# A graph-attention layer with expert feed-forward on one core: the experts' steps get written slots, twelve products of zeros stand ahead of the transposes of the maxima's ends, and the block records start five side steps later

## The chip, the cores and the metric

The kernel runs on one core of a Trainium2 chip. The metric is the device time in microseconds of one execution; less is better. The engines are TensorE (PE; its weight loads are shown as PEld), VectorE (DVE), ScalarE (ACT), GpSimd (POOL) and SyncE (SP). Each works through its own instructions in the order in which the program wrote them, and waits on semaphores for the others.

## The reference

The input is a table `x` of 30000 nodes by 256 features and 510000 edges (`src`, `dst`, a relation of 8 for each), sorted by `dst`. Cut to what matters:

```
xn = layernorm(x)
feat[r, n, h] = xn[n] @ conv_weights[r, h]            # 8 relations, 4 heads of 64
e  = leaky_relu(el[src, type] + er[dst, type])        # one score for each edge and head
m  = segment_max(e, dst);  ex = exp(e - m[dst])
h  = segment_sum(ex / segment_sum(ex) * feat[type, src], dst) + h_bias
x  = x + h
xn = layernorm(x)
gates = softmax(xn @ gW + gb);  top 2 of 4 experts, weights softmaxed again
x  = x + shared_mlp(xn) + sum of the two chosen experts' mlp(xn)
```

## The kernel before

**Stage A** (to about 1740 us) makes `feat`. For each of 235 tiles of 128 nodes it normalizes, transposes, multiplies with all conv weights on TensorE (`group`, L305) and stores the rows to HBM. Beside it runs `side`, a list of generators of which `aside()` advances the first by one `yield`: once a tile while there are three of them, twice a tile afterwards. The second generator, `places` (L490 on), reads the sorted edge records of 12 blocks at a time. Its inner `fetch(k)` issues 12 loads on SP, one for each block, with an address that is read from a register; `fetch(0)` is followed by one `yield`, and after that DVE reads what it brought (`key`, L534).

**Stage B** (about 1740 us to the end) goes over 253 blocks of edges: 252 of 16 times 128 edges, and a last one of 18 times 128. A block covers at most 128 destination nodes. The loop runs over `t` and, inside, over six slots `c`. Work on several blocks is interleaved in the written order of one slot:

- slot 0: loads for block t+2 (SP), the 15 indirect gathers of `feat` rows for block t+1 (POOL, L933; the sixteenth part comes from a stage in HBM), flags for t+1 (ACT copies), the residual of block t-2 (DVE)
- slot 1: two transposes (`pn`) and their copy `through` (ACT), then DVE's `scores(t)`, which ends in two scans that write `fb` (L1033, L1034)
- slot 2: `turn_ends(t)`: TensorE transposes the ends of both scans into the PSUM tile `t1` (L1040, L1041)
- slot 3: `across(t)`: DVE scans over the partitions (L1047, L1048), which reads `t1` and `through`
- slot 4: `turn_back(t)`: two transposes to `t2` (L1055, L1056); DVE's `dest_select(t+2)` (L970)
- slot 5: DVE's `softmax(t)` (L1062 to L1022), ACT's `exps(t)` (L1071, L1072), DVE's first `weigh` of the block (L1079), then `finish(t-1)`: `den` and `ho` (L1104 to L1107) from the PSUM tile `po`

In every slot there are also a part of `sums(t-1)` on TensorE (L1086: one-hot times gathered rows, summed in `po`), a part of `weigh` and `dest_pick` on DVE, of `dest_expand` on TensorE (L987, bf16) and of `onehot` on ACT (L1010, L1011). `po`, `t1`/`pn`/`t2` (one tag, `sm`) and the experts' `pf`/`pw`/`pg` (one tag, `pc`) have one PSUM buffer each.

**The experts.** Four blocks make a group of 512 nodes. When the residual of the fourth is done (slot 0), `Experts.steps()` gives 22 steps: `spread` (ACT's square root, L727), `scale` 0 and 2 (DVE), `turn` 0 and 1 (transposes; ACT copies `xT`, L744), `shared1(0)`, `gates`, `shared1(1)`, four `experts1` (the first holds `choose`, 14 small DVE operations), `shared2`, two `experts2`, two `weigh`, `turn_gates` (transposes the gate weights; ACT copies `wT`, L844), and four `last` (L851 to L854), which need `wT`. Before, the steps go into the list `todo`, and each slot takes one of it: steps 0 to 21 sit in slots 0 to 21 of the 24 slots of four blocks. A step may return a second half; it is kept in `late` and runs at the start of the next slot. So `last(t)` makes the product in one slot, and DVE adds it to `og` (L857) at the start of the next.

Of the kernel before, what the change touches and what calls it, by code (L numbers as in the profile page):

```python
# [11 lines left out]
BF16 = mybir.dt.bfloat16  # L12
# [9 lines left out]
P = 128  # L22
D = 256
R = 8
H = 4
# [15 lines left out]
T = 4  # L41
# [12 lines left out]
def kernel(  # L54
# [26 lines left out]
    nc = tc.nc  # L81
# [94 lines left out]
    for i in range(NPEN + 1):  # L176
        f = wf.tile([P, H, U if i < NPEN else UL], F32, name=f"penf{i}")
# [44 lines left out]
    with ExitStack() as cx:  # L222
# [268 lines left out]
        def places(cl):  # L491
# [19 lines left out]
            def fetch(k):  # L511
                if k == len(batches):
                    return
                b0, n = batches[k]
                rc = rcs[k] = kp.tile([P, GB, UW, 4], I32, name="rcb")
                for b in range(n):
                    lo = nc.values_load(lo_sb[0:1, b0 + b:b0 + b + 1], engines={SP}, min_val=0, max_val=E)
                    r = rec[ds(lo, CAP), :].rearrange("(p u) f -> p (u f)", u=U)
                    nc.sync.dma_start(rc[:, b].rearrange("p u f -> p (u f)"),
                                      bass.AP(tensor=r.tensor, offset=r.offset, ap=[[4 * U, P], [1, 4 * UW]]))  # L520

            fetch(0)
            yield
            done = None
            for k, (b0, n) in enumerate(batches):
                fetch(k + 1)
# [99 lines left out]
        with tc.manual_schedule():  # L626
# [27 lines left out]
            while slot < 16:  # L654
                attention(slot, ab)
                slot += 1
            cl.close()
            side = [edge_records(cl), places(cl), expert_weights()]
            ahead = first_rows()

# [41 lines left out]
    class Experts:  # L702
# [8 lines left out]
        def steps(self):  # L711
# [5 lines left out]
                    + [lambda i=i: self.weigh(i) for i in range(2)]  # L717
                    + [self.turn_gates] + [lambda t=t: self.last(t) for t in range(self.n)])

        def stats(self, t):  # L720
            st = self.pool.tile([P, 6], F32, name="c_st")
            nc.vector.bn_stats(st[:M], self.x1[:M, t, :])
            nc.vector.bn_aggr(self.mv[:M, t, :], st[:M])
# [138 lines left out]
    with ExitStack() as cx:  # L862
        cp = cx.enter_context(tc.tile_pool(name="cb", bufs=1))
# [15 lines left out]
        NCH = 6  # L879
        flat = "p h u -> p (h u)"  # L880
        blk = {}

        class Block:

# [152 lines left out]
        def turn_ends(t):  # L1037
            s = blk[t]
            s.t1 = ps_p.tile([H, 2, P], F32, name="t1", tag="sm")
            nc.tensor.transpose(s.t1[:, 0, :], s.f[:, :, s.u - 1], ident)  # L1040
            nc.tensor.transpose(s.t1[:, 1, :], s.b[:, :, 0], ident)  # L1041

# [44 lines left out]
                                 s.ft[:, u].rearrange("p h d -> p (h d)"), start=u == 0, stop=u == s.u - 1)  # L1087

        groups = {}
        todo = []  # L1090
        late = []

        def put(t, rows_t):

            if t < NBLK:
                n0 = nc.values_load(n0_sb[0:1, t:t + 1], engines={SP}, min_val=0, max_val=N - P)
                nc.sync.dma_start(out[ds(n0, P), :], rows_t)
            else:
                nc.sync.dma_start(out[N - P:N, :], rows_t)
# [9 lines left out]
        def residual_sum(t):  # L1109
            s = blk.pop(t)  # L1110
            q, j = divmod(t, T)
            n = min(T, NBLK + 1 - q * T)
            if j == 0:
                x1 = x1p.tile([P, T, D], F32, name="x1")
                groups[q] = Experts(xc, ph_p, pc_p, x1, n, lambda i, r, q=q: put(q * T + i, r))
            x1 = groups[q].x1
            nc.vector.tensor_add(x1[:, j, :], s.ho.rearrange("p h d -> p (h d)"), s.xt)
            groups[q].stats(j)
            if j == n - 1:
                todo.extend(groups.pop(q).steps())  # L1120

        with tc.manual_schedule():
            for t in range(-2, NBLK + 12):
                def at(f, b, *a):
                    if 0 <= b <= NBLK:
                        f(b, *a)
                for c in range(NCH):
                    while late:  # L1130
                        late.pop()()
                    if c == 0:
                        at(load, t + 2)
                        at(gather, t + 1)
                        at(flags, t + 1)
                    if c == 1:
                        at(flags_across, t + 1)
                    if c == 2:
                        at(turn_ends, t)
                    if c == 3:  # L1140
                        at(across, t)
                    if c == 4:
                        at(turn_back, t)
                    if c == 5:
                        at(softmax, t)
                        at(exps, t)
                    if c < NCH - 1:
                        at(weigh, t - 1, c + 1)
                    if c < 4:
                        at(dest_pick, t + 1, c)  # L1150
                    if c == 0:
                        at(residual_sum, t - 2)
                    if c == 1:
                        at(scores, t)
                    if c == 4:
                        at(dest_select, t + 2)
                    if todo:
                        after = todo.pop(0)()
                        if after:
                            late.append(after)  # L1160
                    if c == 5:
                        at(weigh, t, 0)
                        at(dest_expand, t + 2, 0)
                    if c < 3:
                        at(dest_expand, t + 1, c + 1)
                    at(onehot, t, c)
                    at(sums, t - 1, c)
                    if c == 5:
                        at(finish, t - 1)
            assert not todo and not groups and not late  # L1170


    again = nc.values_load(bad[0:1, 0:1], min_val=0, max_val=1)
# [57 lines left out]
    with ExitStack() as cx:  # L1231
        cp = cx.enter_context(tc.tile_pool(name="cg", bufs=1))
# [128 lines left out]
    with ExitStack() as cx:  # L1361
# [3 lines left out]
        with tc.For_i(0, again * NQ) as q:  # L1365
# [7 lines left out]
            for step in g.steps():  # L1373
                after = step()
# [30 lines left out]
```

## Time and profile before

| what | value |
|---|---|
| median of 10 runs | 6656.92 us (6650.02 to 6666.61) |
| the profiled execution's own time | 6647.23 us |
| its span, first to last instruction | 6645.6 us |
| mean granted TensorE clock | 0.967 |
| busy share: PE, DVE, ACT, POOL | 90%, 81%, 52%, 61% |
| gathers of stage B | 3798, mean 953 ns |
| `sums` products | 8100 instructions, 2214.0 us busy |

"Idle before" is the time that an engine stood ahead of an instruction, and the releaser is the instruction whose semaphore ended it. Granted clock is the share of full speed that the TensorE throttle gave. The profiled execution is 9.7 us shorter than the median.

### The profile page before, as it was taken

To read this page: it belongs to the slowest core of one execution; us is meant where nothing else is said; L and a number is where in the kernel's file an instruction comes from. 1 tells how busy PE (TensorE), PEld (TensorE's weight loads), DVE (VectorE), ACT (ScalarE), POOL (GpSimd) and SP (SyncE) were. 2 spreads that over 40 slices of the span, in tenths; PEclk is the share of its full clock that TensorE was granted. 3 is DMA by queue.
4 is the path that set the end of the run, shared out by engine and by line. 5 is a ranking of instruction groups with operands and counts; after the bars stand their busy time and mean duration, and the time that the engine had idled before them with its cause. 6 is when DMAs were issued, how large, how long until landed. Compare 5 with 4: busy or idle time off the path is not lost. (4 is left out here: it accounts for less than half of the span.)

```text
span 6645.6 us, 96556 instructions
## 1 busy us (share of the span) xinstructions
PE 5978.2 (90%) x25254; PEld 3836.3 (58%) x25255; DVE 5353.9 (81%) x13882; ACT 3428.1 (52%) x9511; POOL 4084.0 (61%) x4327
## 2 busy tenths in 40 slices
PE   9999999999788888888888888888888888888888
PEld 5555555555456566555555565655656555655555
DVE  5555777644588888999999989899999998888886
ACT  2222222222355666665666656666666666566664
POOL 1111111166677777777777777777777777777772
PEclk9999999999899999999999999999999999999998
DMA  6666777799755555555555555555555555555552
GB/s 226 227 211 182 232 234 232 241 342 348 248 154 160 166 161 159 161 157 167 162 160 160 159 161 166 160 161 159 158 167 161 162 158 156 165 159 157 162 156 64
DMA packets 761458, 1209.52 MB, mean 182 GB/s; under 512 B 241639, under 2 KB 599790, under 8 KB 730686
## 3 DMA queue, kind: packets, MB, share of 16 engines
q1 hardware_dynamic: 565453, 663.56, 31.3%
q0 software_dynamic: 194400, 539.40, 29.4%
q8 instruction: 206, 3.38, 0.2%
q14 instruction: 359, 2.93, 0.1%
q10 hardware_dynamic: 1040, 0.26, 0.0%
HBM read 818.57 MB, written 384.23 MB: 181 GB/s over the span
## 5 line engine op out<-in xcount | busy, mean ns | idle before, releaser
L933 POOL DMA_INDIRECT ft<-feat,rk x3798 | 3619.7, 953 | 1198.3 <-issue 465.1
L1086 PE MATMUL po<-ft,oh 128*128 128x260 f32 x8100 | 2214.0, 408 | 153.1 <-DVE ho L1107 139.7
L1086 PEld LDWEIGHTS po<-ft,oh 128*128 128x128 f32 x8100 | 1512.5, 201 | 416.2 <-ACT ends L955 144.3
L305 PE MATMUL ps<-w,xT 128*128 128x448 f32 (+1 forms) x4700 | 1710.2, 519 | 10.5 <-DVE xT L294 8.7
L1079 DVE TENSOR_TENSOR ft<-ft,p 128x768 f32<-128x768 f32 x1518 | 1289.9, 850 | 183.0 <-ACT ft L1072 183.0
L1010 ACT ACTIVATE oh<-icol,rk 128x128 f32<-128x128 f32 x4032 | 1329.1, 389 | 0.0
L305 PEld LDWEIGHTS ps<-w,xT 128*128 128x128 f32 x4700 | 876.4, 191 | 699.6 <-issue 607.9
L307 ACT COPY fo<-ps 128x448 f32<-128x448 f32 (+1 forms) x711 | 378.3, 533 | 1080.6 <-PE ps L305 990.7
L1011 ACT ACTIVATE oh<-oh 128x384 f32<-128x384 f32 x1518 | 740.2, 488 | 48.1
L987 PEld LDWEIGHTS <-ohT 128*128 128x128 bf16 x4050 | 390.9, 158 | 402.0 <-issue 308.4
L1000 DVE TENSOR_REDUCE e<-ere 128x16 f32<-128x384 f32 (+1 forms) x1012 | 561.5, 555 | 34.8
L998 DVE TENSOR_TENSOR ere<-pe,rk 128x384 f32<-128x384 f32 x1008 | 551.7, 547 | 1.3 <-PE pe L987 1.3
L798 PE MATMUL ph<-xT,v 128*128 128x512 f32 (+1 forms) x1024 | 484.3, 596 | 1.0 <-ACT h L799 0.6
L1071 ACT ACTIVATE p<-e 128x64 f32<-128x64 f32 (+1 forms) x253 | 71.2, 281 | 751.9 <-DVE e L1022 742.9
L987 PE MATMUL pe<-erp,ohT 128*128 128x96 bf16 x4050 | 434.0, 232 | 26.1 <-DVE ohT L970 25.5
L307 DVE COPY fo<-ps 128x448 f32<-128x448 f32 (+1 forms) x464 | 242.8, 528 | 211.6 <-PE ps L305 205.8
L294 DVE COPY xT<-ptr 128x256 f32<-128x256 f32 x229 | 97.3, 425 | 368.6 <-PE ptr L292 366.4
L615 POOL DMA_INDIRECT fr<-feat,lowc x252 | 239.9, 952 | 169.2 <-DMA stage<-fr 70.6
L970 DVE TENSOR_SCALAR ohT<-dr,rowid 128x2064 bf16<-128x2064 int16 (+1 forms) x253 | 324.2, 1281 | 3.5 <-DMA feat<-fo 3.0
L274 POOL TENSOR_TENSOR xb<-xg,hb 128x1024 f32<-128x1024 f32 (+1 forms) x59 | 141.9, 2405 | 287.7 <-DMA xg<-in_x_dram 145.3
L851 PE MATMUL pf<-w,h 128*128 128x256 f32 x506 | 169.4, 418 | 148.8 <-ACT wT L844 111.7
L1040 PE MATMUL t<-ident,fb 128*4 128x128 f32 x253 | 69.8, 276 | 237.4 <-DVE fb L1033 237.4
(206 smaller groups left out, 6966.5 us busy)
## 6 DMA issues: line engine op xcount, KB each, us to landing
feat<-fo SPq DMA_DIRECT2D x234, 1040.0 KB
dr<-dk_d SPq DMA_DIRECT2D x252, 516.0 KB
ft<-feat,rk POOLq DMA_INDIRECT x3798
stage<-fr SPq DMA_DIRECT2D x63, 520.0 KB
ft<-stage SPq DMA_DIRECT2D x252, 130.0 KB
xt<-xb_d SPq DMA_DIRECT2D x253, 128.0 KB
out_dram<-og SPq DMA_DIRECT2D x253, 128.0 KB
xb_d<-xb SPq DMA_DIRECT2D x58, 512.0 KB
```

What stands on the lines that cost most here:

```text
L305: nc.tensor.matmul(ps, t["xT"][:, k, :], w[:, k, c0:c1], start=k == 0, stop=k == 1)
L307: eng(t["fo"][:, h0:h1, :HD], ps[:, :n].rearrange("p (a d) -> p a d", d=HD))
L798: nc.tensor.matmul(ps[:, :self.w], lhs, rhs, start=i == 0, stop=i == len(pairs) - 1)
L933: nc.gpsimd.indirect_dma_start(out=s.ft[:, u].rearrange("p h d -> p (h d)"), out_offset=None, in_=feat[:, :], in_offset=bass.IndirectOffse ...
L970: nc.vector.tensor_scalar(ohT[:, :3 * s.dw].rearrange("n (i e) -> n i e", i=3), s.dr[:, :, :s.dw], rowid[:, t:t + 1], None, op0=ALU.is_equal)
L987: nc.tensor.matmul(pe[:, u - u0].rearrange("p f r -> p (f r)"), s.ov[:, u, :], s.erp.rearrange("n h k r -> n (h k r)"), start=True, stop=True)
L998: nc.vector.tensor_mul(ere, s.pe[:, :u1 - u0], s.th[:, u0:u1, None, :].to_broadcast([P, u1 - u0, H * 3, R]))
L1000: nc.vector.tensor_reduce(s.e[:, :, u0:u1].rearrange("p h u -> p u h"), ere.rearrange("p u (h k) r -> p u h (k r)", h=H), AX.X, ALU.add)
L1010: nc.scalar.activation(s.oh[:, u, :], icol, AF.Abs, bias=s.nd[:, u:u + 1])
L1011: nc.scalar.activation(s.oh[:, u0:u1], s.oh[:, u0:u1], AF.Relu, bias=1.0, scale=-1.0)
L1079: nc.vector.tensor_mul(fc, fc, pc[:, :, None].to_broadcast([P, (u1 - u0) * H, HD]))
L1086: nc.tensor.matmul(s.po.rearrange("n h d -> n (h d)"), s.oh[:, u, :], s.ft[:, u].rearrange("p h d -> p (h d)"), start=u == 0, stop=u == s. ...
```

## The change

Three edits. `places` yields six times after `fetch(0)` instead of once. The steps get written slots: step number i of a group runs in slot `SLOTS[i]`, counted from the slot in which the group's fourth residual is made; a group's last four steps fall into the first four slots of the following group, where that group's own step comes first. `late` is now taken from its front. And `turn_ends` first makes twelve products of a 128 by 4 by a 128 by 256 slice of a bf16 tile of zeros into `t1`, which the two transposes then overwrite.

```diff
@@ places
             fetch(0)
-            yield
+            for _ in range(6):
+                yield
@@ class Experts
+        SLOTS = (0, 1, 2, 4, 5, 7, 8, 9, 10, 11, 12, 13, 14, 15, 16, 18, 19, 21, 24, 25, 26, 27)
@@ stage B
+        zeros = cp.tile([P, 2 * P], BF16, name="zeros")
+        nc.vector.memset(zeros, 0.0)
@@ def turn_ends(t)
             s.t1 = ps_p.tile([H, 2, P], F32, name="t1", tag="sm")
+            for _ in range(12):
+                nc.tensor.matmul(s.t1.rearrange("h i p -> h (i p)"), zeros[:, :H], zeros, start=True, stop=True)
             nc.tensor.transpose(s.t1[:, 0, :], s.f[:, :, s.u - 1], ident)
@@ def residual_sum(t)
-                todo.extend(groups.pop(q).steps())
+                first = free[0] = max((t + 2) * NCH, free[0])
+                free[0] += T * NCH
+                for i, f in zip(Experts.SLOTS, groups.pop(q).steps()):
+                    plan.setdefault(first + i, []).insert(0, f)
@@ the loop
                     while late:
-                        late.pop()()
+                        late.pop(0)()
...
-                    if todo:
-                        after = todo.pop(0)()
+                    for f in plan.pop(t * NCH + c, ()):
+                        after = f()
                         if after:
                             late.append(after)
```

More of the change, by code (lines that the diff above doesn't have):

```diff
@@ L1089 @@
         groups = {}
-        todo = []
+        plan = {}
         late = []
+        free = [0]
         def put(t, rows_t):
@@ L1169 @@
                         at(finish, t - 1)
-            assert not todo and not groups and not late
+            assert not plan and not groups and not late
     again = nc.values_load(bad[0:1, 0:1], min_val=0, max_val=1)
```

## The prediction

> **What bounds the kernel now.** First the page's shares, which name no single engine:
>
> ```profile
> PE 5978.2 (90%) x25254; PEld 3836.3 (58%) x25255; DVE 5353.9 (81%) x13882; ACT 3428.1 (52%) x9511; POOL 4084.0 (61%) x4327
> ```
>
> So I read stage B by itself: the instructions of the score line and of the gather line, with their first and last start.
>
> ```profile
> L1027 DVE TENSOR_TENSOR e<-e,ft x253: 259/266/296, 1764.7 to 6563.1; 128x64 f32<-128x64 f32 x126, 128x72 f32<-128x72 f32 x1
> ```
> ```profile
> L933 POOL DMA_INDIRECT ft<-feat,rk x3798: 943/949/1195, 1744.2 to 6542.7; - x200
> ```
>
> The 252 steps from first to last score take 4798.4 us: 19.04 a block, 76.16 a group of four. Next, DVE's waits from 1800 to 6550 us:
>
> ```profile
> DVE ft L1079 <- ACT ft L1072: 180.2, 249, 2.0
> DVE og L857 <- PE pf L854: 77.2, 131, 1.6
> DVE den L1104 <- PE po L1086: 18.7, 59, 0.5
> ```
>
> DVE hardly ever stands. It waits 0.71 once a block for the exponentials, and for TensorE 95.9 us in 62.4 groups: 1.54 a group. With 10.8 us for gathers (0.17) all else is DVE's own work: 76.16 - 1.71 = 74.45 a group. DVE sets the pace, and what can change is its waits. TensorE stands several us a group, but it is in order and its waits end on DVE.
>
> The timeline of one group (slot 0 of the `last` block is 4652.00, of the block before it 4634.01) shows where DVE waits, and what I price with:
>
> ```profile
> 4606.77 0.22 PE L1055 MATMUL t<-ident,carf 4*128 4x4 f32 x1
> ...
> 4607.67 0.59 ACT L744 COPY xT<-ph 128x512 f32<-128x512 f32 x1
> ...
> 4609.71 1.28 ACT L1071 ACT_TABLE_LOAD   x1
> ...
> 4611.31 0.28 ACT L1071 ACTIVATE p<-e 128x64 f32<-128x64 f32 x1 [0.32 <-DVE e L1022]
> ...
> 4659.40 0.60 PE L851 MATMUL pf<-w,h 128*128 128x256 f32 x2
> ...
> 4661.42 0.45 PE L987 MATMUL pe<-erp,ohT 128*128 128x96 bf16 x4
> 4661.52 0.42 DVE L857 TENSOR_TENSOR og<-pf,x 128x256 f32<-128x256 f32 x1 [0.55 <-PE pf L854]
> ...
> 4664.77 0.42 DVE L857 TENSOR_TENSOR og<-pf,x 128x256 f32<-128x256 f32 x1 [0.30 <-PE pf L854]
> ```
>
> POOL is a second floor: in the same timeline gathers start 1.253 apart (0.95 busy, 0.30 of issue), 60 a group, 75.2. Over the stage its 3797 steps need 4758 of the 4798.5 they took. So however short DVE's waits become, the gathers end at most 41 us earlier; the last score, 20.4 after the last gather, could close up by some 15 more.
>
> Last, stage A. TensorE is full there but for one hole:
>
> ```profile
> 575.00:580.00 5.00, 0.00 (x0) 0.00 (x0) 0.12 (x1) 0.00 (x0) 0.00 (x0) 0.63 0.17 33
> 580.00:585.00 5.00, 2.23 (x3) 1.17 (x4) 4.36 (x14) 0.71 (x2) 0.00 (x0) 0.50 0.17 33
> ```
>
> DVE stood 12.43 us ahead of `key` for the records of `fetch(0)`, TensorE 8.66 behind it, and then ran some 10 us at half clock.
>
> **Part one, the yields.** Five more side steps, two a tile of about 7.5 us, put `key` 19 us later than 567.5; the records were there at 579.9. The wait goes: 8.7, and half of 10.2 for the clock, 14 us less. The twelve loads keep SP as before; `fetch(1)` and all of `places` move back by some 11, far from the end of stage A. **-14.**
>
> **Part two, the slots.** DVE's sum stays. Of TensorE's step work one `last` is 2.02 (4659.40 to 4661.42), a 512-column step 1.72. The four `last` move from the third block of a group's 24 slots after the first into the first block of the next group, beside `scale` (0.84 and 0.65 on DVE), `turn`, and the exponential's table load, which follows the square root. The wait for `wT` (1.83 on TensorE, the start of the lateness in the `last` block) goes, since `turn_gates` is now three slots ahead. The half-clock stretches behind that wait go with it: up to 0.6 a group, inside the 1.54.
>
> **Part three, the zeros.** 3036 products, 12 ahead of each transpose. They need `through` of slot 1 to be copied (it is, 1.3 us or more ahead), not `fb`: they hide only while TensorE waits for `fb`. Price of one: the trace has none of this shape. Below stand the bf16 products of 96 columns at 0.058 apart: 12 are 0.70. That row by columns, 0.155, gives 1.86. A 256-column f32 instruction takes 0.216, a 512-column one 0.43, so f32 costs two cycles a column, and the 96-column bf16 row excludes two for bf16. I take half of 0.216: 0.108, **1.3 a block**, nearest to the rows whose width is the same. By the Trainium skill (TensorE: Matmul & The Clock Gate, "Back-to-back issue gap") 256 columns are an estimated 0.109: the same sum.
>
> Now the new block by block, from slot 0, with durations of that timeline.
>
> *First block (`last`, `scale`, `turn`).* The old `last` block reached `turn_ends` at 7.18 (4659.18, the transposes ending at the 4659.40 shown), after waiting for `og`; the zeros make it 8.49. Transposes 0.22, third `last` 2.02: done at 10.73, `og` at 10.83. DVE, with both `scale` now in front, is there at 10.46: waits 0.37. The fourth `last` ends at 13.98, `og` 14.08 against 13.78: waits 0.30. `sums` 1.52, then `turn_back` at 15.5. From `turn_back` to a free ACT the fence above gives 4607.67 - 4606.77 for `turn` to its copy, copy and one-hots to 4609.71, load 1.28: 4.2 in all. ACT is free at 19.7. DVE's `softmax` ends at 14.08 + 0.35 + 0.59 + 1.20 + 1.90 = 18.1. The exponential, covered before by 0.32, now comes 1.55 late, and DVE behind it. Waits **2.2**; without zeros 1.2.
>
> *Second block (`shared1`, `gates`, two `experts1`).* TensorE reaches the zeros at 5.36, the transposes at 6.67 (`fb` allows 6.34), `gates` ends 1.84 later with 0.1 to DVE: 8.83, against 8.21. **0.6**; without zeros 0.2.
>
> *Third block (two `experts1`, `shared2`, `experts2`).* `turn_back` at about 12.9 and its latency make `softmax` wait until 13.05 against 12.52: **0.5**, 0.1 more at `den`; without zeros none.
>
> *Fourth block (`weigh`, `turn_gates`).* TensorE waits for `fb` from 4.3 to 6.9; the zeros hide. None.
>
> Sum 3.4 a group where 1.71 stood: +1.69, times 63 is **+106**. The tail keeps its steps; the last group starts three empty blocks later, which takes no time. +106 - 14 = **+92** on the profiled 6647.2; the median of the runs shown is 9.7 above it, so 6656.9 + 92 is about **6749**.
>
> Two rules bear on this. For the clock the row first, two stretches of 3.4 us in another group (PE busy, PEld, DVE, ACT, POOL, then the granted clock), the first with the wait for `wT`:
>
> ```profile
> 4495.00:4498.40 3.40, 1.61 (x9) 1.07 (x8) 2.49 (x9) 1.12 (x5) 2.72 (x3) 0.97 0.44 109
> 4498.40:4501.80 3.40, 3.40 (x9) 1.89 (x8) 3.30 (x8) 2.41 (x10) 2.48 (x4) 0.53 0.38 100
> ```
>
> A wait of 1.8 us is enough for half clock. The skill's clock page ("Why this matters for your kernels") asks for gaps over about 3 us; by it the zeros would buy no clock, and 0.6 a group (38 us) of my credit would go. And the row of the table load shows 1.28, with the exponential 0.32 after it because of `e`; the skill's ScalarE: Activation LUTs ("What ACT_TABLE_LOAD costs") adds a drain of 1.38, by which the first block would wait 2.9, another 85 us. The measured rows stand in my sum.
>
> **The rivals.** *Faster: the zeros fill waits only.* Place: `turn_back` of the first block. If it starts before 13.9 (zeros near 0, or lateness I overrate), the table load is covered and the slots' gain shows. With the waits of "without zeros", 1.4: -0.3 times 63 - 14 = -34, 6623; with none left POOL's floor holds, -41 - 15 - 14: 6587. For it: TensorE waits for `fb` 0.8 to 2.6 in three of four blocks. Against: these waits stood in other blocks than the `last`. *Cheap zeros,* 0.058 each: waits 1.6, 0.3, 0: +12 - 14, no change, 6655. *Dearer:* at 0.155 the waits are 2.8, 1.2 and 1.1: +181, 6838; a half-clock stretch in the dense first three blocks costs up to 1.7 too, in a third of the groups +36. *The change doesn't do what it says:* zeros held by `through`; then their time would all lie behind `fb`, as in the dearer case.
>
> **How the numbers follow.** Forecast 0.54, with its own range 6690 to 6830; dearer 0.14; faster 0.27; no change 0.05. The range 6595 to 6850 leaves out the floor's end of the faster case and the top of the dearer one. 0.2% (13 us) is about what a measurement of this kernel can tell from no change: faster 0.27, within 0.05, slower 0.68.
>
> **What would show it.** Right: the score line's 252 steps at 19.4 to 19.6 a block; waits for `ft` L1072 near 280 us in total, the long ones once a group; `turn_ends` ahead of the `og` waits; no hole at 575 us; POOL with more gaps. Wrong: those waits unchanged while TensorE's idle time shrinks, or zeros closer than 0.1 us apart.

## The result and the profile after

The changed kernel takes 6913.7 us (median of 8 runs, 6912.0 to 6916.9), the kernel before in the same comparison 6662.7 (28 runs, 6648.8 to 6671.3): ratio 1.0380, 95% interval [1.0371, 1.0389]. It is 251 us slower. The forecast had the direction and much too little of the size: +92, and 6913.7 lies outside its range.

The profiled execution of after took 6913.83 us, span 6912.1, at a granted clock of 0.984, higher than the 0.967 of before. First the page's shares, and the group of the zeros:

```profile
PE 6230.2 (90%) x28290; PEld 4004.3 (58%) x28291; DVE 5352.3 (77%) x13883; ACT 3435.3 (50%) x9511; POOL 4068.3 (59%) x4327
L1049 PE MATMUL t<-zeros 128*4 128x256 bf16 x3036 | 373.3, 273 | 0.1
```

DVE's sum is that of before (5353.9), its share is lower: the added time is DVE standing. The 273 ns is the mean length of one product's record; the records overlap, and in the trace the zeros start 0.109 us apart (median).

The score line and the gather line of stage B, with first and last start:

```profile
L1034 DVE TENSOR_TENSOR e<-e,ft x253: 259/265/330, 1752.9 to 6828.7; 128x64 f32<-128x64 f32 x126, 128x72 f32<-128x72 f32 x1
```
```profile
L940 POOL DMA_INDIRECT ft<-feat,rk x3798: 940/946/1167, 1732.5 to 6801.8; - x200
```

252 steps take 5075.8 us, 20.14 a block or 80.6 a group, where 19.04 and 76.2 stood. Stage B starts 11.8 earlier, and the gathers, which need 4758, took 5069: they no longer press. The same two windows of stage A show why the start is earlier; TensorE has no hole there any more:

```profile
575.00:580.00 5.00, 5.00 (x17) 2.75 (x16) 2.04 (x6) 1.68 (x4) 0.00 (x0) 1.00 0.52 181
580.00:585.00 5.00, 5.00 (x16) 2.64 (x15) 1.66 (x7) 1.28 (x3) 0.00 (x0) 1.00 1.04 404
```

DVE's waits from 1800 to 6800 us (total us, times, longest), 62.1 groups:

```profile
DVE ft L1089 <- ACT ft L1082: 362.6, 248, 2.3
DVE g L769 <- PE pg L755: 105.4, 62, 2.9
DVE og L862 <- PE pf L859: 48.2, 122, 0.6
DVE c L1072 <- PE t L1066: 35.7, 61, 0.6
```

In a group that is 5.84 for the exponentials, of which 4 times 0.71 was there before, 1.70 for the gates (new), 0.78 for `og` and 0.57 for `softmax` (new). Take the 6.05 above the old 2.84 from 80.6 and 74.5 is left, the 74.45 of the prediction. So the whole loss is in these rows, and the first is the largest. The timeline of one group's first block shows what it is made of:

```profile
5075.74 1.47 PE L1049 MATMUL t<-zeros 128*4 128x256 bf16 x12
5077.14 0.27 PE L1050 MATMUL t<-ident,fb 128*4 128x128 f32 x1
...
5079.48 0.42 DVE L862 TENSOR_TENSOR og<-pf,x 128x256 f32<-128x256 f32 x1 [0.41 <-PE pf L859]
...
5082.73 0.42 DVE L862 TENSOR_TENSOR og<-pf,x 128x256 f32<-128x256 f32 x1 [0.30 <-PE pf L859]
...
5084.13 0.22 PE L1065 MATMUL t<-ident,carf 4*128 4x4 f32 x1
...
5085.04 0.58 ACT L749 COPY xT<-ph 128x512 f32<-128x512 f32 x1 [7.65 <-PE ph L747]
...
5086.55 0.22 DVE L1029 TENSOR_REDUCE e<-m 128x4 f32<-128x64 f32 x1
...
5087.08 1.28 ACT L1081 ACT_TABLE_LOAD   x1
...
5088.38 0.28 ACT L1081 ACTIVATE p<-e 128x64 f32<-128x64 f32 x1
...
5088.99 0.95 DVE L1089 TENSOR_TENSOR ft<-ft,p 128x768 f32<-128x768 f32 x1 [2.22 <-ACT ft L1082]
...
5090.95 1.90 PE L1096 MATMUL po<-ft,oh 128*128 128x260 f32 x6 [2.78 <-ACT ends L962]
```

`softmax` is done at 5086.77 (5086.55 + 0.22), the exponential starts at 5088.38. ACT had stood 7.65 us in front of `xT`, which waits for the products of the `turn`; one-hots and the exponential's table load queue behind that copy. I call the distance from the end of `softmax` to the start of the exponential the lateness: 1.61 here; in the kernel before its median is 0.03 in every block.

The queue on ACT is not new. In the kernel before, the second `turn` copy and the table load stood ahead of this exponential too, as the prediction's fence shows, and the end of `softmax` there is

```profile
4611.05 0.22 DVE L1022 TENSOR_REDUCE e<-m 128x4 f32<-128x64 f32 x1
```

Counted from the start of `turn_back`'s transposes (4606.77 before, 5084.13 now), the load ends after 4.22 before and 4.23 now, but `softmax` after 4.50 before and 2.64 now. DVE was the later of the two and hid ACT's queue; now it is not. With the change the four `last` stand in this block: the fourth holds DVE up (`og`, 0.30 of standing) and stands ahead of `turn_back` on TensorE. No run moves the `last` steps alone, so their part is read from the timelines and not tested.

With DVE late, `den` and `ho` are late, and TensorE stands 2.78 at the border to the second block (the releaser named is `ends`, which these products do not read; `ho`, which frees `po` for them, ended 0.26 earlier). Then the clock (PE, PEld, DVE, ACT, POOL busy, granted clock, DMA share, GB/s):

```profile
5088.00:5091.00 3.00, 0.22 (x4) 0.12 (x2) 1.94 (x5) 2.92 (x12) 2.09 (x4) 1.00 0.98 238
5091.00:5094.40 3.40, 3.40 (x10) 2.14 (x11) 3.30 (x8) 1.66 (x5) 2.73 (x3) 0.65 0.86 278
5094.40:5097.80 3.40, 3.40 (x15) 1.84 (x14) 3.19 (x11) 1.60 (x5) 2.55 (x3) 0.85 0.42 111
```

A stretch of 3.4 us at half clock lies across the last two windows. 41 such stretches fall on the 63 borders to a second block, and a group with one lasts 81.3 us, one without 79.6 (medians).

The third block has a second late exponential, with another cause:

```profile
5127.05 0.69 ACT L830 ACTIVATE a<-ph,c 128x512 f32<-128x512 f32 x1
...
5127.64 0.61 ACT L834 COPY wide<-wt 128x512 f32<-128x512 f32 x1
5127.73 0.22 DVE L1029 TENSOR_REDUCE e<-m 128x4 f32<-128x64 f32 x1
...
5129.59 0.26 ACT L1081 ACTIVATE p<-e 128x64 f32<-128x64 f32 x1
...
5130.20 0.95 DVE L1089 TENSOR_TENSOR ft<-ft,p 128x768 f32<-128x768 f32 x1 [2.25 <-ACT ft L1082]
```

Slot 16 is the fifth slot of the third block, and SLOTS puts the second `experts2` there: its relu (0.69) and `wide` (0.61) with the one-hots behind them go ahead of the exponential, which starts 1.64 late.

### The profile page after: what moved, and what is told of

Read it like the earlier page. It is cut to its first block, busy times and chain, and to the rows that moved or that the text cites. A ratio compares the mean times of both kernels' runs of the same rounds, so it can differ in the third digit from the quotient of the medians.

```text
span 6912.1 us, 102332 instructions
## 1 busy us (share of the span) xinstructions
PE 6230.2 (90%) x28290; PEld 4004.3 (58%) x28291; DVE 5352.3 (77%) x13883; ACT 3435.3 (50%) x9511; POOL 4068.3 (59%) x4327
## 5 line engine op out<-in xcount | busy, mean ns | idle before, releaser
L1096 PE MATMUL po<-ft,oh 128*128 128x260 f32 x8100 | 2162.4, 401 | 376.0 <-ACT ends L962 172.6
L1096 PEld LDWEIGHTS po<-ft,oh 128*128 128x128 f32 x8100 | 1462.1, 194 | 752.4 <-ACT ends L962 355.8
L994 PE MATMUL pe<-erp,ohT 128*128 128x96 bf16 x4050 | 419.1, 227 | 93.4 <-DVE ohT L977 87.1
L1049 PE MATMUL t<-zeros 128*4 128x256 bf16 x3036 | 373.3, 273 | 0.1
L804 ACT ACTIVATE h<-ph,b 128x512 f32<-128x512 f32 x192 | 130.9, 682 | 440.0 <-PE ph L803 437.2
L1049 PEld LDWEIGHTS <-zeros 128*4 128x4 bf16 x3036 | 237.1, 84 | 147.5 <-issue 85.2
L749 ACT COPY xT<-ph 128x512 f32<-128x512 f32 (+1 forms) x128 | 74.6, 583 | 492.5 <-PE ph L747 492.5
```

The source lines that it names most:

```text
L994: nc.tensor.matmul(pe[:, u - u0].rearrange("p f r -> p (f r)"), s.ov[:, u, :], s.erp.rearrange("n h k r -> n (h k r)"), start=True, stop=True)
L1049: nc.tensor.matmul(s.t1.rearrange("h i p -> h (i p)"), zeros[:, :H], zeros, start=True, stop=True)
L1096: nc.tensor.matmul(s.po.rearrange("n h d -> n (h d)"), s.oh[:, u, :], s.ft[:, u].rearrange("p h d -> p (h d)"), start=u == 0, stop=u == s. ...
```

## The experiments

**Theories.** A: in the written slots, ScalarE work that waits for TensorE holds up two exponentials that stand behind it (the `turn` in slots 4 and 5, whose first copy is ahead of the exponential of slot 5; the second `experts2` in slot 16); the late exponential of the first block lengthens TensorE's wait at the border, and half clock follows; the zeros cost what TensorE needs for them besides. B: the zeros are the cost; what is late is late because they hold TensorE back. C: any layout in slots costs, the zeros are free.

On three of the chips the kernel before itself took 8371 to 8441 us, with a stall once a group that the last section shows; what is read from those runs is the ratio to the kernel before on the same chip, and whether the exponentials are late; by how much they are late in the third block varies there.

### Where the kernel before takes about 6660 us

| kernel | zeros | `turn` in slots | second `experts2` in | us, median | ratio, 95% | first, second, third, fourth block |
|---|---|---|---|---|---|---|
| before | none | old order | old order | 6657.7 | 1 | 18.83, 19.82, 18.31, 19.19 |
| changed_again | 12 | 4, 5 | 16 | 6911.8 | 1.0379 [1.0362, 1.0397] | 21.80, 21.62, 19.54, 17.70 |
| turn_late_b | 12 | 5, 6 | 16 | 6756.5 | 1.0142 [1.0125, 1.0159] | 20.29, 20.59, 19.51, 17.70 |
| act_late_b | 12 | 5, 6 | 17 | 6683.9 | 1.0036 [1.0023, 1.0049] | 20.29, 20.59, 18.36, 17.71 |
| changed_nz_b | none | 4, 5 | 16 | 6776.5 | 1.0173 [1.0156, 1.0190] | 21.04, 21.01, 18.77, 17.70 |
| act_late_nz | none | 5, 6 | 17 | 6583.4 | 0.9881 [0.9865, 0.9898] | 19.55, 20.63, 17.59, 17.71 |

The last column is the mean step in us from one block's first `fb` scan to the next one's, over blocks 16 to 239, by the block's place in its group. The steps of before are those of its profile above. `turn_late_b` and `changed_nz_b` ran on a chip where the kernel before took 6661.7, the others where it took 6657.7.

**The changed kernel again** (no edit).

> The changed kernel itself, beside the others of this call. Where the kernel before takes 6660 us, every theory has it at about 6914 us (ratio 1.038). Where the kernel before takes 8371 us: theory A (ScalarE work put ahead of the exponentials in slots 4 and 16) has it 60 to 190 us above the kernel with that work moved one slot on (8431 us), so 8490 to 8620; theory B (the zeros themselves) has it level with that one, 8420 to 8445.

6911.8, 254 more than the kernel before beside it: the loss repeats.

**Both moves** (slots, zeros and yields else as changed):

```diff
-        SLOTS = (0, 1, 2, 4, 5, 7, 8, 9, 10, 11, 12, 13, 14, 15, 16, 18, 19, 21, 24, 25, 26, 27)
+        SLOTS = (0, 1, 2, 5, 6, 7, 8, 9, 10, 11, 12, 13, 14, 15, 17, 18, 19, 21, 24, 25, 26, 27)
```

> The changed kernel, zeros and yields kept, with the turn one slot later (slots 5 and 6) and the second half of the experts one slot later (17), so that ScalarE's xT copies, and its relu and wide, stand behind the exponentials of the first and third block. Theory A: against the changed kernel of this call 1.5 us less in each of two blocks of 63 groups, 190 us less (6720 us where the changed one takes 6914), and the exponentials' waits in the first and third block go from 1.5 us to under 0.2. Theory B: level with the changed kernel, within 30 us.

6683.9, 228 us less; theory A had 190. Lateness goes from 1.61 to 0.03 in the first block and from 1.64 to 0.34 in the third. By blocks: 1.51 less in the first, 1.03 in the second, 1.18 in the third; 3.72 times 63 is 234. DVE's waits in its stage B (1800 to 6550 us, 61.7 groups):

```profile
DVE ft L1089 <- ACT ft L1082: 190.9, 247, 1.2
DVE og L862 <- PE pf L859: 49.2, 121, 0.6
DVE g L769 <- PE pg L755: 36.0, 60, 0.7
DVE c L1072 <- PE t L1066: 33.3, 61, 0.7
```

The exponentials are down to 3.1 a group, near the four times 0.71. The gates went from 1.70 to 0.58, though none of the second block's own steps was moved (the second `turn` came into its first slot). The `og` and `softmax` rows, those of the zeros, stand as they were. Theory B, which had the two kernels level, falls.

**The turn alone, one slot later** (slots 5 and 6; 16 stays).

> The changed kernel with the turn alone one slot later, again. Where the kernel before takes 6660 us, theory A: 1.51 us a group less in the first block and 1.03 in the second, 6752 us; rival (the half-clock stretch does not follow from the late exponential of the first block): 6817 us. Where the kernel before takes 8400 us: 70 to 80 us less than with the second half of the experts moved alone, as in the call before.

6756.5, theory A's 6752 and not the rival's 6817: the first block gives 1.51, and the second 1.03 although it got a step more. The first block in this kernel, seen from ACT:

```profile
4976.35 1.28 ACT L1081 ACT_TABLE_LOAD   x1
4984.31 0.28 ACT L1081 ACTIVATE p<-e 128x64 f32<-128x64 f32 x1 [6.67 <-DVE e L1029]
...
4984.79 0.59 ACT L749 COPY xT<-ph 128x512 f32<-128x512 f32 x1
```

The load now runs 8 us early, since no copy that waits stands ahead of it; DVE waits 0.71 for this exponential. At the border TensorE waits 1.22 where it waited 2.78, and at most one half-clock stretch is left at the 63 borders where there were 41:

```profile
4986.94 1.55 PE L1096 MATMUL po<-ft,oh 128*128 128x260 f32 x6 [1.22 <-ACT ends L962]
```

One move took both away. It also brings the second `turn`'s transposes into the second block's first slot, but ahead of these products as before: TensorE's own work from `turn_back` to the wait takes 4.08 here and 4.03 in the changed kernel, while `ho` ends 5.04 after `turn_back` here and 6.55 there (medians). So the wait shrinks by what the exponential was late, and the half clock goes with it. The zeros have no part in this wait: it is 2.78 in the next kernel too, with 41 half-clock stretches.

**The changed kernel without its zeros.**

```diff
-        zeros = cp.tile([P, 2 * P], BF16, name="zeros")
-        nc.vector.memset(zeros, 0.0)
...
-            for _ in range(12):
-                nc.tensor.matmul(s.t1.rearrange("h i p -> h (i p)"), zeros[:, :H], zeros, start=True, stop=True)
```

> The changed kernel without its zeros, again. In every run so far with the turn in slots 4 and 5, zeros or not, the first block's exponential starts 1.60 us after its input is there, 0.03 where the turn is one slot later. Theory A: 1.4 us a group for that in the first block, 1.2 for the third, and the half-clock stretch where TensorE stands long enough: 6740 to 6815 us where the kernel before takes 6660. Theory B (without the zeros TensorE has the time to take the lateness up): 6583 to 6620.

6776.5, inside theory A's 6740 to 6815. The lateness is 1.61 and 1.53 without a single product of zeros. It does not need them: DVE stands for the product of the fourth `last` without them too (0.11, with them 0.30), so DVE and ACT both run behind TensorE, and in both kernels `softmax` ends 2.64 after the start of `turn_back` and the table load 4.23 (medians).

**Both moves and no zeros.**

> The kernel with the turn and the second half of the experts one slot later, and no zeros. Against the same with zeros: theory A has the zeros at 12 x 0.11 = 1.3 us of TensorE a block of which most lies in its waits, so 0 to 40 us less; theory B has them on the path, 12 x 0.11 x 252 = 330 us less.

6583.4 us, 100 less than with zeros: between theory A's 0 to 40 and theory B's 330. Of A's numbers this is the one that was off: the zeros cost more than it allowed here, and nearer to what the prediction had for them (below). It is also the fastest kernel of the study, 1.2% under the kernel before. The parts overlap and are not shares of the 251: the moves alone give back 228, leaving out the zeros alone about 138, both together 328, and the slots and yields that remain are worth 74 against the kernel before. What it waits for (1800 to 6550 us, 62.9 groups):

```profile
DVE ft L1084 <- ACT ft L1077: 195.7, 251, 1.4
DVE g L769 <- PE pg L755: 14.9, 63, 1.7
...
DVE og L862 <- PE pf L859: 4.2, 3, 2.1
```

The `og` waits, 77.2 us in the kernel before, are gone, and its gathers are at their floor:

```profile
L938 POOL DMA_INDIRECT ft<-feat,rk x3798: 942/947/1159, 1734.1 to 6500.0; - x200
```

3797 steps in 4765.9 us are 1.255 each, against the 1.253 at which they follow each other in the timeline of before.

**The old order, with the gates' weights turned early.** Yields as changed, no zeros, steps in one slot after the other as before, but `turn_gates` beside the step of slot 12.

```diff
+        SLOTS = (0, 1, 2, 3, 4, 5, 6, 7, 8, 9, 10, 11, 12, 13, 14, 15, 16, 12, 18, 19, 20, 21)
```

> No zeros; the six yields; the experts' steps in slots that are one after the other as in the kernel before, but the gates' step taken out of its place and put into slot 12, beside another. Theory A: the steps stand in the order that left the exponentials on time, so none of the 1.5 us waits; what the kernel before waits for at the experts' gates goes: 6590 to 6640 us where the kernel before takes 6660, bounded below by the gathers of GpSimd, 75.2 us a group. Theory C (any layout of the experts' steps in slots costs): 6800 us or more.

6638.2 us, ratio 0.9962 [0.9945, 0.9979]. Theory C falls, with this kernel and the one above: written slots as such cost nothing. Theory A's time is met, but not for its reason, since the early gates bring nothing either. The step is 19.06 a block against 19.04, and DVE's `og` waits are 79.0 us where they were 77.2; TensorE's 109.7 us of waiting for `wT` turned into waiting for `ho` (215.8 from 135.4). Most of what it gains is the yields' earlier start (first scan 1754.3 against 1766.0).

### Where the kernel before takes 8371 to 8441 us

| kernel | ratio to before, 95% | lateness, first block | lateness, third block |
|---|---|---|---|
| yields_only | 0.9983 [0.9974, 0.9993] | stall in it | 0.03 |
| slots_only | 0.9933 [0.9916, 0.9950] | 1.60 | 1.51 |
| slots_only_b | 0.9949 [0.9933, 0.9965] | 1.60 | 1.65 |
| zeros_only | 1.0233 [1.0216, 1.0250] | 0.03 | 0.03 |
| zeros_only_b, zeros_only_c | 1.0249 [1.0220, 1.0278], 1.0204 [1.0176, 1.0233] | 0.03, 0.03 | 0.03, 0.03 |
| zeros6 | 0.9925 [0.9908, 0.9942] | 1.60 | 0.49 |
| act_late | 1.0071 [1.0048, 1.0094] | 0.03 | 0.03 |
| border_zeros | 1.0137 [1.0108, 1.0166] | 1.61 | 0.92 |
| turn_late | 1.0077 [1.0051, 1.0103] | 0.03 | 0.50 |
| relu_late | 1.0170 [1.0142, 1.0197] | 1.60 | 0.03 |
| changed_nz | 0.9913 [0.9886, 0.9939] | 1.60 | 1.73 |

(medians in us, by the block's place in its group)

The first block's column sorts the kernels: 1.60 wherever the `turn` is in slots 4 and 5, with 12, 6 or no zeros, and 0.03 wherever it is not. The zeros alone, in the old order, make no exponential of the first or third block late; there they do so in the second, by 1.5 to 2.0.

**The yields alone, the slots alone, the zeros alone** (each one hunk of the change), and the change with six zeros (`range(6)` for `range(12)`).

> The kernel before with the six yields alone. Theory A (the yields only take away the hole at 575 us): stage A is shorter by 8.7 us of standing and about 5 us of half clock, 14 us in all; about 6648 where the kernel before has 6662. Rival: the wait turns up again at a later batch, no change.

> The kernel before with the written slots alone, no zeros, one yield. Theory A (what costs is ACT work that the slots put in front of the exponentials in slot 4 of a block: turn's copy and the table load in the first block, experts2's two operations in the third): the exponentials are still 1.2 us late in the first block and 1.4 in the third, gates 0.2, so 2.8 a group for 1.7 before: 70 us slower, up to 140 with half clock behind the long block border; 6730 to 6800. Rival B (the zeros are the cost): as before or faster, 6600 to 6660. Rival C (the slots are all of it, the zeros hide): 6925, as the changed kernel without its 14 us.

> The kernel before with the twelve products of zeros alone, in the old order of the steps. Theory A: TensorE waits 1.2 to 2.8, 1.5 and 1.0 us for fb in three of the four blocks, which hides most of 1.3 each; only the block of the last steps pays, 1.3 us, less up to 0.6 for half clock: 20 to 80 us slower, 6680 to 6740. Rival B (the zeros are the cost): 250 us slower, 6910. Rival C (the zeros hide): within 15 us.

> The changed kernel with six products of zeros for twelve. Theory A: the exponentials stay as late (their chain hangs on the slots), og, gates and softmax waits fall by about 1 us a group: 60 us faster than the changed kernel, 6850. Rival B (cost in proportion to the zeros): half of the way, 6790. Rival C: no change, 6914.

The yields are worth 0.17% of 8371, 14 us. The slots alone make those chips' kernel faster, and six zeros on top of slots and yields leave it there (0.9925), while twelve without the slots make it 2.3% slower. Taken alone this spoke for theory B. But the stall sits in the first block in the old order and in the second in the slotted one, so the slots' ratio holds the stall's move too. With the zeros alone it stays in the first block; their 2.0 to 2.5% (170 to 210 us) is above theory A's 20 to 80, later 90 to 140, and some 1.7 of 3.3 us a group (against the yields alone) lies in the second block, whose exponential is late there. How much of that hangs on the stall is open.

**The same two again, the moves, and twenty more zeros at the border.** The last adds to the changed kernel, with its 12 zeros, in the slot where the second block begins:

```diff
+                    if c == 0 and t % T == 2 and 6 <= t <= NBLK:
+                        zt = ps_p.tile([H, 2, P], F32, name="zt", tag="sm")
+                        for _ in range(20):
+                            nc.tensor.matmul(zt.rearrange("h i p -> h (i p)"), zeros[:, :H], zeros, start=True, stop=True)
```

> The written slots alone, no zeros, one yield, against the kernel before on one chip. Theory A (ACT work that the slots put in front of the exponentials): exponentials 1.2 us late in the first block, 1.4 in the third, gates 0.2: 2.8 a group for 1.7: +70 us, up to +140 with half clock behind the longer block border. Rival B (the zeros are the cost): no slower than before. Rival C (the slots are all of it): +265.

> The zeros alone in the old order of the steps. Theory A: three of four blocks hide most of their 1.3 us behind fb, the block of the last steps pays: +20 to +80 us. Rival B (the zeros are the cost): +250. Rival C (they hide): within 15 us.

> The changed kernel, zeros and yields kept, with three entries of SLOTS moved: turn to slots 5 and 6, the second experts2 to slot 17, so that their ACT operations come behind the exponentials of slot 5. Theory A: the exponentials come on time in the first and third block (2 times 1.5 us a group) and the block border, with its half clock in two of three groups (1.1), shrinks: 4.1 a group, 260 us faster than the changed kernel, about the time of the kernel before. Rival B (TensorE is simply late by the zeros): those waits only move to den and softmax, at most 50 us faster.

> The changed kernel plus twenty more products of zeros once a group, ahead of the sums of slot 6, where TensorE stands 2.8 us for ho. Theory A's second part (that standing brings half clock in two of three groups, which makes gates late by 1.7): the clock stays full, 1.1 a group: 70 us faster than the changed kernel although there is more work. Rival: the clock falls for another reason, no change, or slower by the products that do not fit.

The first two repeat to within 0.16%. `act_late` shows the two moves to do what they should for the exponentials, and `border_zeros` is inconclusive: the second block, whose clock it was to hold, is the one with the stall there (38.8 us), and the changed kernel itself did not run on that chip.

**The moves one by one, no zeros, zeros alone.** `relu_late` is the changed kernel with slot 17 for 16 only.

> The changed kernel with the turn alone one slot later (slots 5 and 6), the second half of the experts left in slot 16. Theory A, with TensorE's half-clock stretch in the second block a follower of the late exponential of the first: 1.51 us a group less in the first block and 1.03 less in the second, 160 us in all, so 6752 us where the changed one takes 6912; the third block's exponential stays 1.5 us late. Rival (the half-clock stretch comes from the gates or the zeros): 1.51 us less in the first block only, 6817 us.

> The changed kernel with the second half of the experts alone one slot later (17), the turn left in slots 4 and 5. Theory A: the third block's exponential is on time, 1.18 us a group less, 74 us in all, so 6838 us where the changed one takes 6912, and the half-clock stretch in the second block stays. Rival: as much as the turn's move or nothing, within 30 us of 6912.

> The changed kernel without its zeros, slots and yields kept. Theory A (ScalarE's order alone makes the exponentials late): 6583 us, the time with both moves and no zeros, and 2.4 to 3.7 us a group on it, so 6730 to 6815. Theory B (the zeros hold TensorE back and so make the exponentials late): within 30 us of 6583.

> The kernel before with the zeros alone. Where the kernel before takes 6660 us, theory A has the zeros at about what they cost with the two moves made, 1.5 us a group, so 6750, and more where a transpose of the experts waits behind them, up to 6800. Theory C (slots all of it, zeros free): 6650 to 6680.

The lateness answers each as theory A has it: the `turn`'s move mends the first block and leaves the third late (0.50 here, 1.64 in `turn_late_b`), the relu's move mends the third alone. The times are not read further here; the two that mattered most were run again where the stall is absent, and stand above. What zeros alone cost the old order without the stall was not measured.

## Why the prediction was wrong

**Held.** DVE sets the pace and keeps its 74.45 a group: 74.5. The yields: -14 forecast, 11.8 by the first score. Their 5 us for the clock was misread: the half-clock stretch of before runs from 576.27 to 586.51, and TensorE stood until 582.77, so 3.7 us of its work lay in it, worth 1.9. A zero was put at 0.108 from the f32 row of its width; 0.109 measured, which is also the estimate from the Trainium skill (TensorE: Matmul & The Clock Gate, "Back-to-back issue gap"). The waits for `og`, 0.37 and 0.30: 0.41 and 0.30. The first block's exponential, 1.55: 1.51 (2.22 - 0.71), and 1.51 us a group came back when it was mended; that the exponential was covered before and would not be now is what the traces show. `softmax` of the third block, 0.5: 0.57 a group. Fourth block, none: its step is 17.7 with and without zeros. The exponential started 0.02 after its table load's end (5087.08 + 1.28, then 5088.38), so the drain of 1.38 of the Trainium skill (ScalarE: Activation LUTs, "What ACT_TABLE_LOAD costs") does not show, and leaving it out was right. And where the "faster" rival ended, at 6587 with no wait left and POOL's floor holding, is where the kernel with both moves and no zeros is, 6583.4; it gets there by leaving the zeros out, not by hiding them.

**Failed, first: "Third block ... 0.5, 0.1 more at `den`".** The step followed `softmax`'s input and stopped there. It did not go on to ask what ACT has queued ahead of the exponential in that block, as it had in the first. The second `experts2` puts a relu and `wide` there. 1.54 (2.25 - 0.71) a group, some 97 us by DVE's waits, was put at nothing. Moving that step alone out of the way, from `turn_late_b` to `act_late_b`, gave back about 71 us (1.0142 - 1.0036, of 6660); 0.3 of lateness stayed.

**Failed, second: "Second block ... 0.6".** Where no half-clock stretch falls on it, the gates' wait is 0.61. With one it is near 2.3; the mean of all is 1.70. The stretch was in the text, as part of the dearer rival, "up to 1.7, in a third of the groups": the size was right and the share was two thirds. The step that would have given the share was at hand: the 1.55 at the exponential passes through `den` and `ho` to TensorE's border wait, 2.78, and the text had itself shown a wait of 1.83 with half clock behind it. 1.1 a group, 69 us.

The sum with both: 92 + 97 + 69 = 258, against 251 measured.

**The dearer rival** does not come out of its own terms: 2.8 + 1.2 + 1.1 is 5.1 a group, 3.39 over the 1.71, so +200 and 6857 and not +181 and 6838. The measured time lies above both, and not by dearer zeros.

**"Without zeros 1.2" for the first block.** The forecast had the exponential later with the zeros than without them. It is 1.6 late either way, since the fourth `last` sets DVE's time as well as TensorE's, and DVE's waits for the exponentials in the changed order without zeros (357.9 us in 60.6 groups, 5.9 a group) are those of after. For the zeros themselves the forecast had 3.4 - 1.4 = 2.0 a group, 126 us; the kernels with both moves differ by 100, with `og` falling from 49.2 to 4.2 us, `softmax`'s row from 33.3 to 0.8 and the gates' from 36.0 to 14.9, and in the changed order the zeros cost 138 (1.0380 - 1.0173, of 6660). So the zeros' term was about right, and the zeros were not what was missing.

**The signs.** `turn_ends` stood ahead of the `og` waits, the hole at 575 us was gone, and POOL had more gaps, as said; the score line's step is 20.14 instead of 19.4 to 19.6, and the waits for `ft` are 363 us instead of near 280, because the long ones come twice a group and not once.

**The two cases of the clock.** The Trainium skill (TensorE: Matmul & The Clock Gate, "Why this matters for your kernels") asks that TensorE have no gaps over about 3 us. Here waits of 2.78 were followed by half clock at 41 of 63 borders, and waits of 1.22 in `turn_late_b` at one of 63 at most, so less than 3 us was enough. The zeros did buy clock: half-clock time in stage B is 171 us with them and 468 without in the changed order, 27 and 300 with both moves. It bought no time, since the kernels without zeros are the faster ones. In the changed order without zeros, 222 of the 468 us lie in the fourth block, whose step is 17.70 either way; behind those at the border to the second block the gates' wait is 0.82, without one 0.16.

## What to carry to other kernels

When steps are moved by hand, list for every place the instructions of each engine's queue that come to stand ahead of the ones others wait for, and do it for every block, not only for the one that looks full: putting two steps with ScalarE work one slot later gave back 228 us. Ask also what hides such a queue today: here the same copy and table load stood ahead of the exponential before, and cost nothing as long as DVE came later still. In these traces the table load stands in ACT's queue directly ahead of the exponential, so a copy that waits for TensorE in front of it holds back the load too. And when a wait is forecast on one engine, follow it to the next one's border and ask what the clock does there.

## What the runs showed that was not expected

On three chips the kernel before took 8371, 8371 and 8441 us, in all runs, profiled or not. Stage A is as long there (first scan at 1766.1 with the slots alone, 1766.0 in the kernel before elsewhere). In stage B what TensorE releases stands for up to 22 us once a group, in the kernel with the yields alone in the first block:

```profile
5010.74 0.56 DVE L999 TENSOR_TENSOR ere<-pe,rk 128x384 f32<-128x384 f32 x1 [7.52 <-remote]
...
5020.64 0.58 ACT L745 COPY xT<-ph 128x512 f32<-128x512 f32 x1 [21.60 <-remote]
```

`remote` means that the profile names no instruction as the releaser. The products that this copy needs are shown as done at 5001.69. SyncE's instructions, mostly 0.02 to 0.4 us long elsewhere, follow each other there in steps of 0.70 us, and the gathers pause too; durations on DVE and ACT are unchanged, and no instruction fetch falls into the stretch. With the steps in slots the stall moves to the second block, at the gates. Its cause stays open.
